# The upper triangle of the decay matrix: select by position on GpSimd in place of a clamp on VectorE

## The chip, the cores and the metric

The kernel runs on one core of one Trainium2 chip. The metric is the device time of one execution in microseconds (us). The engines are named as in the profile: PE (TensorE; PEld its weight loads), DVE (VectorE), ACT (ScalarE), POOL (GpSimd) and SP (SyncE, which issues all DMAs here).

## The reference

Input x is [64, 256, 256] (64 samples of 256 tokens of 256 channels), all in float32. Four layers follow one another, each added to x after a layer norm: a graph attention network with two attention layers (gnn0), a feed-forward block on the 127 best-ranked of 256 tokens (ffn0), another graph attention (gnn1) and a Mamba-2 block (ffn1). The change lies in the last one. With one chunk of 256 tokens its core is

```python
cs = cumsum(dt * A)                       # per head, over the 256 tokens
Lmat[l, s] = exp(cs[l] - cs[s]) if l >= s else 0
Y[l] = sum over s of (C[l] . B[s]) * Lmat[l, s] * x[s] * dt[s]
```

for 8 heads of 64 channels; B and C are shared by the heads. Above the diagonal (l < s) Lmat is zero. There cs[l] - cs[s] is positive and can be large, so that exp of it, if it were taken, could overflow.

## The kernel before

Two samples form a group, so there are 32 groups. The work of a group is cut into lanes, written as Python generators; a step of a lane is what lies between two `yield`s. Lane a is gnn0, b is ffn0 and then gnn1, c is ffn1. The first group's gnn0 is done by halves (lanes a and d, one sample each), and so is the last group's ffn1 (lanes e and f). Lane w loads and prepares weights. Three strings of letters give the order in which the steps are issued: FIRST (305 letters, the start), ORDER (199 letters, repeated 29 times; in each repetition lanes a, b and c of different groups advance by one group), and LAST (403 letters, the end). A letter whose lane can't begin yet is skipped; when LAST's letters have given out, the remaining steps are taken from the lanes in turn. Each engine works through its own instructions in the order of issue.

In ffn1, E holds for each head a tile of 128 partitions (s within a half of the tokens) by 3 blocks of 128 columns (l) per sample: block 0 is s and l in the first half, block 1 is s in the first half and l in the second, block 2 is both in the second. So blocks 0 and 2 hold the diagonal, and block 1 lies wholly below it. E is made as follows:

- cs is written to DRAM (csd) and read back, spread over all partitions (`spread_row`, L809, 264 DMAs). Six buffers of E take turns.
- `decays(h)` clamps blocks 0 and 2 to the value on the diagonal, min(cs[l], cs[s]), with one instruction on DVE (L820; ccs is cs by partition). Then ACT takes exp(E - cs[s]) (L826, two instructions per sample).
- B C^T comes from PE into PSUM (pb), and DVE moves it to cb with a product by tri3 (L891), which is 1 where l >= s and 0 elsewhere.
- DVE multiplies E by cb (L899), and PE takes E into py.

Where the clamp acted, exp gives 1, and tri3's zero in cb removes it.

The convolution of ffn1 is a chain for each m in (4, 0, 1, 2, 3): PE (pp), ACT (L841), three instructions on DVE (L845), ACT (th, L850), DVE (L851); `decays(m)` comes after m = 0 to 3. Later, in the rounds m = 0 to 3, follow L899 for two heads, pz (PE), gz (ACT L907, DVE L908), py (PE), L924 on DVE, L925 on POOL, and for m = 0 and 1 `decays` of two more heads (4 to 7). Other lines that the text names: L489 copies transposed attention weights (at) from PSUM on ACT, L496 and L499 are exps of gnn0 on ACT, L473 scales attention weights on POOL, L567 and L750 are additions on POOL, L671 and L674 are products on DVE in ffn0's gelu, ahead of py there, L594 and L393 are an addition and statistics on DVE. Line numbers of matmuls and transposes are those of two helpers, L251 and L254.

Of the kernel before, what the change touches and what calls it, by code (L numbers as in the profile page):

```python
# [12 lines left out]
ALU = mybir.AluOpType  # L13
AX = mybir.AxisListType

P = 128
# [2 lines left out]
GELU_C = 0.7978845608028654  # L19
GELU_A = 0.044715  # L20
FIRST = (
    "dwddadadwaaadawdaaddadaddaaaaadddaaddaaaaddaddaddadaaadaddaddwawdaaaaaaadddadddawdaaaaadadaadaddbaba"
    "aaabaaaabbaawaaaabwaabaaaaababbbaabbbwababababbbbabaaaabaabaawabababbaaaaabbbaaabbbbabbbaababbababab"
    "baababbbaaaabbabbbabbbaaacwccaababcaababbaabcaaabaaabacabbabbbbbaaabaabaabcbcabaabwbbaacabbaabawabca"
    "bbbab"
)
ORDER = (
    "cAaaccbbbbbbacabaccccbccaabacccabcbccabaacbccacabcaaaacacacbcccccbcacabcccbcaaacacbbccccccacaaccbcac"
    "cbacacabccabcccbcbBabccaccbcccabbcacaacbaccacbcbaacbcbbcbcababcbbcbCccbbbbaacaacabcaabbcbbabbbbbccc"
)  # L30
LAST = (
    "ececefefceecbbceccbbcbffbbbccfcbbfceccebbfcccbefccbcbeceebfcccecccecccceccfbccbcecccbccbeeccbefceccf"
    "ccccccfeeebbccecccfecffffcccfbffebcccbfbceffbccbcccefebbcefcccfceeebcbccccbfefccbcccbfbffcbbccccbcbb"
    "cfceefcbfbbcfefcbbcffbfecccbfcbfefbbbfbfbccffeeeebffbeccccfffebbfebbefbecfcbccccccbcbbcbffcccbeeceec"
    "ebfecbbbbcebffcceccbccccbeccebccececbbefcccffecfccffccfecfebcebceeceecebcffbcfeccfffcfecfeccefcececc"
    "cfe"
)


# [1 line left out]
def kernel(ctx: ExitStack, tc: tile.TileContext, a: dict, out: bass.AP):  # L41
# [5 lines left out]
    nc = tc.nc  # L47
    x = a["x"]
    B, N, D = x.shape
# [19 lines left out]
    def psum(name):  # L69
        return ps.tile([P, 512], F32, tag="ps", name=name)  # L70

    def cons(name, *shape, dt=F32):
        return const.tile(list(shape), dt, tag=name, name=name)
# [16 lines left out]

    ident = cons("ident", P, P)
    make_identity(nc, ident)

    tri3 = cons("tri3", P, 3 * P)
    nc.gpsimd.memset(tri3, 1.0)
    for blk in (0, 2):
        nc.gpsimd.affine_select(
            out=tri3[:, blk * P : (blk + 1) * P],
            in_=tri3[:, blk * P : (blk + 1) * P],
            compare_op=ALU.is_ge,  # L100
            fill=0.0,
            base=0,
            pattern=[[1, P]],
            channel_multiplier=-1,
        )

    before = cons("before", P, 2, N, dt=BF16)
    nc.gpsimd.memset(before, 1.0)
    for c in range(2):
        nc.gpsimd.affine_select(  # L110
            out=before[:, c, :],
            in_=before[:, c, :],
            compare_op=ALU.is_gt,
            fill=0.0,
            base=c * P,
            pattern=[[-1, N]],
            channel_multiplier=1,
# [8 lines left out]
    ones = cons("ones", P, 32)  # L126
# [110 lines left out]
    def tiled(pool, shape, tag, name, bufs):  # L237
        return pool.tile(list(shape), F32, tag=tag, name=name, bufs=bufs)
# [7 lines left out]
    def sized_sm(tag, n, most, *rest, bufs=4):  # L246

        return sm(tag, P, most, *rest, bufs=bufs)[:, :n]
# [117 lines left out]
    def sized(G, own=None):  # L366
# [3 lines left out]
        def wide(make, tag, *rest):  # L370

            if own is None:
                return make(tag, *rest)
            i = taken[tag] = taken.get(tag, -1) + 1
            if i == len(shared.setdefault(tag, [])):
                shared[tag].append(make(tag, *rest))
            return shared[tag][i]
# [374 lines left out]
        def ffn1(xt, of):  # L752
# [6 lines left out]
            r0 = 32 * (own or 0)  # L759
            mine = slice(own or 0, (own or 0) + G)  # L760
            pd = psum("pd")
            for k in range(KD):
# [6 lines left out]
            R = 32 * G  # L769
            dtT, dz, csT = (  # L770
                wide(lambda t: tiled(big, (64, N), t, t, 1), t)[r0 : r0 + R] for t in ("dtT", "dz", "csT")
            )
# [5 lines left out]
            yield  # L778
            nc.vector.scalar_tensor_tensor(dtT, dtT, 0.0, dz, ALU.max, ALU.add)
            nc.vector.tensor_scalar(dz, dtT, negA[r0 : r0 + R], None, ALU.mult)  # L780
            nc.vector.tensor_tensor_scan(csT, tri3[r0 : r0 + R, P : P + 1].to_broadcast([R, N]), dz, 0.0, ALU.mult, ALU.add)


            csd = wide(lambda t: rowd.tile([NH, 2, 3 * P], F32, tag=t, name=t), "csd")[:, mine]
# [11 lines left out]
            ccs = sized_sm("ccs", G, 2, 2, NH, bufs=2)  # L796
# [17 lines left out]
            def decays(h):  # L814

                yield

                e = es[h]
                diag = e.rearrange("p b (k l) -> p b k l", k=3)[:, :, ::2, :]
                nc.vector.tensor_tensor(  # L820
                    diag, diag, ccs[:, :, :, h : h + 1].to_broadcast([P, G, 2, P]), ALU.min
                )
                yield
                for b in range(G):
                    for half, to in enumerate((slice(0, N), slice(N, N + P))):
                        nc.scalar.activation(e[:, b, to], e[:, b, to], AF.Exp, bias=ncs[:, b, half, h : h + 1])  # L826
# [7 lines left out]
            for m in (KI, *range(KI)):  # L834
                yield
                pp = psum("pp")
                for k in range(KD):
                    mm(pp[:, :T], W_in[:, k, DI + m * P : DI + (m + 1) * P], xT[k][:, :T], start=(k == 0), stop=(k == KD - 1))
                yield
                s, pp = columns("xs", "xs"), pp[:, :T]  # L840
                nc.scalar.activation(s, pp, AF.Identity, bias=conv_b[:, m : m + 1], scale=conv_w[:, m, 3:4])  # L841
                s3 = s.rearrange("p (b t) -> p b t", b=G)
                p3 = pp.rearrange("p (b t) -> p b t", b=G)
                for d in range(1, 4):
                    nc.vector.scalar_tensor_tensor(  # L845
                        s3[:, :, d:], p3[:, :, : N - d], conv_w[:, m, 3 - d : 4 - d], s3[:, :, d:], ALU.mult, ALU.add
                    )
                yield
                th = columns("m", "th")
                nc.scalar.activation(th, s, AF.Tanh)  # L850
                nc.vector.scalar_tensor_tensor(s, th, 1.0, s, ALU.add, ALU.mult)  # L851
                xs[m] = s
                if 0 <= m < 4:
                    yield from decays(m)
# [23 lines left out]
            cb = wide(lambda t: tiled(big, (P, 2, 3 * P), t, t, 1), "cb")[:, mine]  # L878
            yield

            pb = [psum("pb") for _ in range(G)]
# [6 lines left out]
                    )  # L888
            yield
            for b in range(G):  # L890
                nc.vector.tensor_tensor(cb[:, b, :], pb[b][:, : 3 * P], tri3, ALU.mult)  # L891
            cb2 = cb.rearrange("p b l -> p (b l)")

            ys = []
            for m in range(KI):
# [16 lines left out]
                for b in range(G):  # L912
                    for half in range(2):
                        for q in range(2):
                            h = 2 * m + q
# [11 lines left out]
                for h in (2 * m + 4, 2 * m + 5):  # L927
                    if len(es) < NH:
                        spread_row()
                    if h < NH:  # L930
                        yield from decays(h)
# [23 lines left out]
            for c in range(C):  # L955
# [5 lines left out]
                nc.vector.scalar_tensor_tensor(xt[:, c, :], po[:, :D], r[:, c : c + 1], xt[:, c, :], ALU.mult, ALU.add)  # L961

        return {f.__name__: f for f in (moments, gnn0, ffn0, gnn1, ffn1)}

    both, one = sized(2), [sized(1, half) for half in range(2)]
# [116 lines left out]
```

## Time and profile before

| | |
|---|---|
| Median of 3 runs | 3652.24 us (3652.19 to 3652.80) |
| Profiled execution: time, span from the first to the last instruction | 3653.81 us, 3652.1 us |
| Mean granted TensorE clock | 0.99 |
| PE busy | 3533.4 us, 97% |
| DVE busy | 2842.1 us, 78% |
| ACT busy | 2189.1 us, 60% |
| POOL busy | 1146.8 us, 31% |
| DMA, mean | 41 GB/s |

Busy times are summed over one profiled execution. PE's instructions are pipelined and their ends are modelled, so a busy PE isn't one at its peak. A stretch of the profile is read by its windows (busy time of each engine in it), by its waits (which engine stood idle, and what ended that), and by the timeline (instructions in order of time, like ones merged, with the idle time before them in brackets).

### The profile page before, as it was taken

What the parts mean: (1) busy time and instruction counts of PE and PEld (TensorE: products, weight loads), DVE (VectorE), ACT (ScalarE), POOL (GpSimd) and SP (SyncE); (2) the same over time, 40 slices, a digit from 0 to 9 for tenths busy, and PEclk for the clock granted to TensorE, in tenths of its full rate; (3) what the DMA queues carried; (4) which work ended last, traced back from release to release, by engine and by line L of the source; (5) the groups of instructions that cost most, each with busy time, mean ns of one, the idle gap of its engine ahead of it and who ended that gap; (6) DMA issues with size and microseconds to landing.
All of it is one profiled execution on the core that took longest, in us unless ns stands there. A gap on an engine that the chain in (4) does not pass through costs nothing.

```text
span 3652.1 us, 50662 instructions
## 1 busy us (share of the span) xinstructions
PE 3533.4 (97%) x17004; PEld 2550.6 (70%) x17004; DVE 2842.1 (78%) x7275; ACT 2189.1 (60%) x4942; POOL 1146.8 (31%) x1274
## 2 busy tenths in 40 slices
PE   8999999999999999999999999999999999999876
PEld 6766776776776776776776776776776777776544
DVE  5577778777778777878777878777878777878776
ACT  4565665665665665666665666655666655666544
POOL 2223333323333323333323333323333323333222
PEclk9999999999999999999999999999999999999989
DMA  3011101111101111101111101111101111101111
GB/s 116 1 39 43 49 15 43 48 42 46 49 15 43 48 40 48 49 15 43 48 40 49 48 16 43 49 40 49 44 20 43 48 40 49 41 23 37 43 43 48
DMA packets 90260, 150.89 MB, mean 41 GB/s; under 512 B 12304, under 2 KB 57232, under 8 KB 90000
## 3 DMA queue, kind: packets, MB, share of 16 engines
q1 hardware_dynamic: 90000, 147.65, 12.1%
q8 instruction: 135, 2.21, 0.2%
q14 instruction: 125, 1.02, 0.1%
HBM read 125.86 MB, written 17.56 MB: 39 GB/s over the span
## 4 chain that ended last, share of the span: by engine, by line
PE 81%; DVE 12%; ACT 4%; issue 1%; POOL 1%; DMA 1%; SPq 0%; ACTq 0%; POOLq 0%; DVEq 0%
PE pp L251 31%; PE u L251 10%; PE py L251 9%; PE po L251 7%; PE pz L251 6%; PE pt L254 5%; PE ph L251 4%; PE pa L251 3%; PE psel L251 2%; DVE st L393 1%; DVE xt L595 1%; DVE g L674 1%; DVE w L498 1%; DVE g L671 1%; DVE w L594 1%; PE pss L251 1%
## 5 line engine op out<-in xcount | busy, mean ns | idle before, releaser
L251 PE MATMUL pp<-W_fc,o 128*128 128x256 f32 (+1 forms) x2048 | 460.1, 379 | 0.4 <-DVE W_fc L286 0.4
L845 DVE SCALAR_TENSOR_TENSOR xs<-pp,conv_w,xs 128x510 f32<-128x510 f32 (+5 forms) x495 | 359.9, 728 | 93.9 <-ACT xs L841 79.9
L251 PEld LDWEIGHTS pp<-W_fc,o 128*128 128x128 f32 x2048 | 381.9, 189 | 67.8 <-issue 15.9
L826 ACT ACTIVATE E<-E,ncs 128x256 f32<-128x256 f32 (+1 forms) x1024 | 382.0, 449 | 61.0 <-DVE E L820 58.3
L473 POOL TENSOR_SCALAR e<-e,den 128x256 f32<-128x256 f32 x384 | 186.8, 505 | 714.2 <-PE pp L251 350.3
L251 PE MATMUL pp<-xT,W_in 128*128 128x512 f32 (+1 forms) x660 | 303.6, 593 | 0.0
L850 ACT ACTIVATE th<-xs 128x512 f32<-128x512 f32 (+1 forms) x165 | 101.7, 617 | 326.6 <-DVE xs L845 311.4
L925 POOL TENSOR_TENSOR xs<-xs,gz 128x512 f32<-128x512 f32 (+1 forms) x132 | 205.9, 1561 | 203.0 <-DVE xs L924 200.5
L251 PE MATMUL py<-w,g 128*128 128x256 f32 x1024 | 236.2, 383 | 20.7 <-DVE g L674 20.7
L899 DVE TENSOR_TENSOR E<-E,cb 128x768 f32<-128x768 f32 (+1 forms) x264 | 250.5, 964 | 1.1
L705 POOL TENSOR_TENSOR xt<-xn,xt 128x512 f32<-128x512 f32 x64 | 81.3, 1270 | 526.1 <-DVE xn L702 525.9
L251 PE MATMUL pz<-xT,W_in 128*128 128x512 f32 (+1 forms) x528 | 242.8, 583 | 0.0
L567 POOL TENSOR_TENSOR o<-w,o 128x512 f32<-128x512 f32 (+1 forms) x132 | 180.7, 1369 | 197.8 <-DVE w L501 197.8
L251 PE MATMUL ph<-sel,w 128*128 128x256 f32 x1024 | 242.0, 379 | 0.0
L251 PE MATMUL po<-W_ol,xs 128*128 128x256 f32 x1024 | 241.3, 379 | 0.0
L251 PEld LDWEIGHTS py<-w,g 128*128 128x128 f32 x1024 | 190.0, 190 | 70.9 <-DVE g L674 46.7
L251 PE MATMUL pp<-xT,mlp_w 128*128 128x512 f32 (+1 forms) x528 | 236.5, 583 | 0.7 <-ACT xT L419 0.7
L251 PE MATMUL u<-at,h 128*128 128x256 f32 x1024 | 236.8, 379 | 0.0
L251 PE MATMUL pp<-o,mlp_w 128*128 128x512 f32 (+1 forms) x528 | 231.1, 590 | 2.9 <-POOL o L567 2.9
L820 DVE TENSOR_TENSOR E<-E,ccs 128x512 f32<-128x512 f32 (+1 forms) x264 | 224.3, 863 | 0.0
L393 DVE BATCH_NORM_STATS2 st<-xt 128x6 f32<-128x256 f32 x512 | 185.1, 413 | 49.7 <-POOL xt L750 23.4
L251 PEld LDWEIGHTS u<-at,h 128*128 128x128 f32 x1024 | 191.7, 190 | 37.6 <-issue 7.3
(179 smaller groups left out, 7722.3 us busy)
## 6 DMA issues: line engine op xcount, KB each, us to landing
E<-csd SPq DMA_DIRECT2D x248, 384.0 KB
xt<-in_x_dram SPq DMA_DIRECT2D x31, 512.0 KB
out_dram<-xt SPq DMA_DIRECT2D x31, 512.0 KB
cs<-xs SPq DMA_DIRECT2D x64, 64.0 KB
E<-csd SPq DMA_DIRECT2D x16, 192.0 KB
w<-in_L_ffn_w_dram SPq DMA_DIRECT2D x2, 1024.0 KB
W_in<-in_L_ffn_W_in_dram SPq DMA_DIRECT2D x1, 1160.0 KB
mlp_w<-in_L_gnn_mlp_w_dram SPq DMA_DIRECT2D x2, 512.0 KB
```

The source lines that it names most:

```text
L251: nc.tensor.matmul(to, lhsT, rhs, start=start, stop=stop)
L254: nc.tensor.transpose(to, of, eye)
L393: nc.vector.bn_stats(st[:, c, :], xt[:, c, :])
L473: nc.gpsimd.tensor_scalar(e, e, den[:, c : c + 1], 1.0, ALU.mult, ALU.mult)
L567: nc.gpsimd.tensor_tensor(o1[m], w, o1[m], ALU.add)
L705: nc.gpsimd.tensor_tensor(pair(xt, b), xn[b], pair(xt, b), ALU.add)
L820: nc.vector.tensor_tensor(diag, diag, ccs[:, :, :, h : h + 1].to_broadcast([P, G, 2, P]), ALU.min)
L826: nc.scalar.activation(e[:, b, to], e[:, b, to], AF.Exp, bias=ncs[:, b, half, h : h + 1])
L845: nc.vector.scalar_tensor_tensor(s3[:, :, d:], p3[:, :, : N - d], conv_w[:, m, 3 - d : 4 - d], s3[:, :, d:], ALU.mult, ALU.add)
L850: nc.scalar.activation(th, s, AF.Tanh)
L899: nc.vector.tensor_tensor(e2, e2, cb2, ALU.mult)
L925: nc.gpsimd.tensor_tensor(yt, yt, gz, ALU.mult)
```

## The change

After it, `decays(h)` issues on POOL, for each sample of the group, one `affine_select` on blocks 0 and 2 of E: where l - s is negative, E becomes -3e38, whatever it was; elsewhere it stays. The exp of that is 0, so cb needs no triangle: L891 becomes a plain copy from PSUM. The tile tri3 and its set-up on POOL go, and the scan that makes cs takes its ones from the tile `ones`. The number of steps in each lane stays, but FIRST, ORDER and LAST hold their letters in another order.

```diff
 FIRST = (
...
 ORDER = (
-    "cAaaccbbbbbbacabaccccbccaabacccabcbccabaacbccacabcaaaacacacbcccccbcacabcccbcaaacacbbccccccacaaccbcac"
-    "cbacacabccabcccbcbBabccaccbcccabbcacaacbaccacbcbaacbcbbcbcababcbbcbCccbbbbaacaacabcaabbcbbabbbbbccc"
+    "Acaccbbbabbcabacccccaccbbbcccaccbcacacaabbcabcacccaaccabbaacacaccccbcbccacbaaccacbacccccacacbaccaaac"
+    "bacabcabcccabcccbacacbBbccbcccccababacbacaacccbbcbabcabccbbabbcbbacbCbbcbcaacaacabcbaabbcbabbbbbccc"
 )
 LAST = (
...
-    tri3 = cons("tri3", P, 3 * P)
-    nc.gpsimd.memset(tri3, 1.0)
-    for blk in (0, 2):
-        nc.gpsimd.affine_select(
-            out=tri3[:, blk * P : (blk + 1) * P],
-            in_=tri3[:, blk * P : (blk + 1) * P],
-            compare_op=ALU.is_ge,
-            fill=0.0,
-            base=0,
-            pattern=[[1, P]],
-            channel_multiplier=-1,
-        )
...
-            nc.vector.tensor_tensor_scan(csT, tri3[r0 : r0 + R, P : P + 1].to_broadcast([R, N]), dz, 0.0, ALU.mult, ALU.add)
+            nc.vector.tensor_tensor_scan(csT, ones[r0 : r0 + R, :1].to_broadcast([R, N]), dz, 0.0, ALU.mult, ALU.add)
...
                 diag = e.rearrange("p b (k l) -> p b k l", k=3)[:, :, ::2, :]
-                nc.vector.tensor_tensor(
-                    diag, diag, ccs[:, :, :, h : h + 1].to_broadcast([P, G, 2, P]), ALU.min
-                )
+                for b in range(G):
+                    nc.gpsimd.affine_select(
+                        out=diag[:, b], in_=diag[:, b], compare_op=ALU.is_ge, fill=-3e38, base=0,
+                        pattern=[[0, 2], [1, P]], channel_multiplier=-1,
+                    )
...
             for b in range(G):
-                nc.vector.tensor_tensor(cb[:, b, :], pb[b][:, : 3 * P], tri3, ALU.mult)
+                nc.vector.tensor_copy(cb[:, b, :], pb[b][:, : 3 * P])
```

More of the change, by code (lines that the diff above doesn't have):

```diff
@@ L21 @@
 FIRST = (
[L22 to L25, printed above, removed]
+    "waaadadddwaadadddaddadaaaaaawdddwaddadaaaaddaddaaadadaaaddddaadaaddaaaddadaddddaaadaaaadaaddadwbaabb"
+    "aaaaawaaaawabaabaaabaaabbaaaaaabbabaabbwbbaaaabaabbbaabbawbbbabbaabaaabaaaaaabwbbbbaabbbbabbbabaaaab"
+    "bbbbbaabaabbbbbabbababbaaabaaabbcbaaaaaabaaaababaaaabbbacwabacacaababwacbbcawacbbbaaabcbaababbcbbaba"
+    "bbbbc"
 )
 ORDER = (
-    "cAaaccbbbbbbacabaccccbccaabacccabcbccabaacbccacabcaaaacacacbcccccbcacabcccbcaaacacbbccccccacaaccbcac"
-    "cbacacabccabcccbcbBabccaccbcccabbcacaacbaccacbcbaacbcbbcbcababcbbcbCccbbbbaacaacabcaabbcbbabbbbbccc"
+    "Acaccbbbabbcabacccccaccbbbcccaccbcacacaabbcabcacccaaccabbaacacaccccbcbccacbaaccacbacccccacacbaccaaac"
+    "bacabcabcccabcccbacacbBbccbcccccababacbacaacccbbcbabcabccbbabbcbbacbCbbcbcaacaacabcbaabbcbabbbbbccc"
 )
 LAST = (
[L32 to L36, printed above, removed]
+    "eefecfebcbecbfeffbecfbcccbcbceccbbcbccfcefbeeccbbcfccbeecccbeececcebcfbccccccfcccfffecebbeccceccbecc"
+    "cfccffbeccfccecccccbcfcceccbcbbeeccfccbbfcbceccebccfcbcebeecfcbffeecbcccccbfcfbbffcbbceffbfbccebcfbe"
+    "bbceefecbcbfbcfcecbcfcbefbbbebfbffceeccefcceeecbfccefbefebfcfccccbbbfbeebefbfcfeccebcbfffccfcfffbeff"
+    "fccbfcecbcbfebccccbcceeccbcccbeecfebeecbbcbcccccbfccccccbbebecefcfcbfccfcbccefcffcfcefecfececcefecfe"
+    "ccf"
 )
```

## The prediction

> **What bounds the kernel now.** I read the page's busy shares and slices first, then the windows, the waits of PE, the groups by form, and the timeline of the last 250 us.
>
> ```profile
> PE 3533.4 (97%) x17004; PEld 2550.6 (70%) x17004; DVE 2842.1 (78%) x7275; ACT 2189.1 (60%) x4942; POOL 1146.8 (31%) x1274
> PE   8999999999999999999999999999999999999876
> PEclk9999999999999999999999999999999999999989
> ```
>
> PE is full in 36 of 40 slices. The four others are the first and the last three, and in the last ones the clock falls too. The windows give sizes (us, then PE, PEld, DVE, ACT, POOL busy, clock, DMA):
>
> ```profile
> 1228.60:1338.33 109.73, 108.78 (x529) 78.65 (x529) 87.68 (x224) 67.81 (x153) 35.83 (x39) 1.00 0.12 41
> 2325.93:2435.67 109.74, 108.79 (x529) 78.65 (x529) 87.66 (x224) 67.80 (x153) 35.84 (x39) 1.00 0.12 40
> 3423.26:3460.00 36.74, 24.11 (x109) 15.24 (x107) 33.17 (x78) 19.85 (x51) 7.65 (x9) 0.81 0.07 22
> 3500.00:3540.00 40.00, 26.70 (x101) 17.13 (x101) 30.80 (x64) 16.66 (x36) 5.62 (x7) 0.85 0.05 17
> 3580.00:3620.00 40.00, 21.50 (x98) 17.15 (x96) 29.68 (x72) 19.53 (x42) 0.00 (x0) 0.79 0.24 77
> ```
>
> The program is a period of 109.73 us, 29 times over (ORDER), between a head of some 240 us and a tail of some 230. In a period PE idles 0.95 us and DVE 22. Over the tail's 229 us (3423 to the end) PE is busy for 163, the three rows above are its idlest, and in them DVE is the fullest engine. Who makes PE wait within one period:
>
> ```profile
> PE py L251 <- DVE g L674: 0.6, 1, 0.6
> PE pst L254 <- ACT ss L944: 0.2, 1, 0.2
> PE pd L251 <- ACT xT L419: 0.2, 1, 0.2
> ```
>
> None of the three is the clamp (L820), so a period has at most 0.95 us to give, 27.6 us over 29. Now what the change exchanges, from the groups by form, and the nearest row of the new operation, from the groups of POOL (the mean in ns stands behind the busy time):
>
> ```profile
> L820 DVE TENSOR_TENSOR E<-E,ccs 128x512 f32<-128x512 f32 x248 | 216.9, 885 | 0.0
> L891 DVE TENSOR_TENSOR cb<-pb,tri 128x384 f32<-128x384 f32 x64 | 32.5, 547 | 0.4 <-PE pb L251 0.3
> L473 POOL TENSOR_SCALAR e<-e,den 128x256 f32<-128x256 f32 x384 | 186.8, 505 | 714.2 <-PE pp L251 350.3 <-ACT w L496 169.7 <-DVE den L468 138.9
> L110 POOL TENSOR_SCALAR_AFFINE_SELECT before<-before 128x256 bf16<-128x256 bf16 x2 | 0.8, 404 | 0.0
> ```
>
> The clamps cost DVE 217 us, and POOL's own row for a select of 256 columns is 404 ns. Last, one round of the two half groups' convolutions in the tail, from the timeline:
>
> ```profile
> 3600.74 0.42 ACT L850 ACTIVATE th<-xs 128x256 f32<-128x256 f32 x1 [1.01 <-DVE xs L845]
> 3601.18 0.42 DVE L851 SCALAR_TENSOR_TENSOR xs<-th,xs 128x256 f32<-128x256 f32 x1 [0.21 <-ACT th L850]
> 3601.53 0.75 DVE L820 TENSOR_TENSOR E<-E,ccs 128x256 f32<-128x256 f32 x2
> 3601.98 1.49 ACT L826 ACTIVATE E<-E,ncs 128x256 f32<-128x256 f32 x4 [0.83 <-DVE E L820]
> 3603.38 1.00 ACT L841 ACTIVATE xs<-pp,conv_b,conv_w 128x256 f32<-128x256 f32 x2
> 3603.96 2.94 DVE L845 SCALAR_TENSOR_TENSOR xs<-pp,conv_w,xs 128x255 f32<-128x255 f32 x6 [1.68 <-ACT xs L841]
> ```
>
> Here the clamp is on the path: ACT waits 0.83 for it, and the next convolution waits for ACT.
>
> **The change, part by part.** *Totals.* 264 clamps (224.3 us) leave DVE. POOL gets 31 x 8 x 2 + 16 = 512 selects of 128x256. A select costs 0.40 (the bf16 row) to 0.51 (f32, another operation): I take 0.42, by the select's own row, 215 us, or 6.7 a period. POOL goes from 35.8 to some 42.5 of 109.73, DVE from 87.7 to some 80.5. Neither was the bound, so in the periods this is worth nothing by itself: PE's 108.78 cover it.
>
> *cb, scan, set-up.* A copy of 384 columns lies between L690's 0.417 (256 columns from PSUM) and today's 0.547, and an input fewer gives no reason for a loss. I take 0.50: 3 us of DVE under PE, 0.3 in the tail. The scan reads ones in place of tri3: nothing. The set-up loses a memset (0.42) and two selects of 0.30 on POOL before 3 us, while DVE waits for x until 4.27: nothing.
>
> *The new chain.* A select needs only E's DMA, not L851 or ccs, so for heads 0 to 3 it can be done before ACT asks. It waits for that DMA at the head of POOL's queue, with L925, L567, L473 and L750 behind it; DVE's clamp stood there with no idle time before it (0.0 in its row), so E was in place, and I add nothing. SP's DMAs keep their number and sizes. For heads 4 to 7 the code issues the select behind L925 on POOL, which waits for L924. The exps that wait for it hold up what is queued on ACT: gz (L907) and the copies L489, and PE waits for those.
>
> *Tail, half groups.* The letters of LAST give out before this stretch in both versions, and the remaining steps run f, e in turn, so the order is the same. In the round above the exps can start when th ends, 3601.16 for 3601.98: 0.82. Two gaps between convolutions gain that; the first gains 0.3, as its E lands at about 3595.7; behind the fourth the path is PE's transposes. Sum -1.9. In the rounds of m, L924 to L924 takes 5.62 (3621.25 to 3626.87), with the first exp 1.60 after L924. With the change: L924 0.55, two L925 of 0.70, a select 0.42 and a step of 0.1 are 2.47, so +0.87 in each of two rounds: +1.7. Bounds 1.6 and 2.9, the upper one if L899, which would then run at that time, slows L925 as it does elsewhere (1.80 in place of 1.28). What is late next is ACT's eight exps (3.05).
>
> *Tail, last two whole groups.* Convolutions of group 30 start at 3499.73, 3506.77, 3513.90 and 3521.62. L851 (0.60) and L820 (0.61) leave the path between th and exps: 0.6 a gap if DVE's queue remains the limit, 1.2 if not. I take 0.9 x 3 = 2.7 there, and 2.2 for group 29, where DVE is 90% busy. Bounds of both together 3.6 and 7.2. Their rounds of m get the later exps (+1.3 at most a round, two each). In group 29's PE has no wait above 0.2 from 3446.8 to 3466.9, which hides it; without that cover it is 2.6. I take +0.7 for group 30's.
>
> *Head.* No clamp starts before 236.9. FIRST is another order of the same steps, and PE idles 23 us there: 0, bounds -2 and +2.
>
> *Sum.* -1.9 + 1.7 - 2.7 - 2.2 + 0.7 - 0.3 = -4.7. With the bounds: about -11 to +5. The profiled execution took 3653.81 (span 3652.10 and 1.7 around it), 1.6 above the median of 3652.24. Against the median: 3647.5. The clock that the tail's rows show (0.79 to 0.85) is taken as it is.
>
> **A rule against it.** Where L820 ran beside L925, the clamp took up to 1.77 against 0.68 alone, and L925 1.66 against 1.28; the two L899 that I found beside one-input L473 took 0.951 against 0.949 alone. So I add nothing for L899 beside selects, outside the rivals. The Trainium skill (SBUF — State Buffer, Who interferes with whom) says that a DVE instruction with two SBUF inputs and a GpSimd instruction that reads SBUF exclude each other, and that the first holds for its whole length. The trace agrees only in part: at 1259.48 the clamp started 0.16 before L925 and still took 1.69. By the rule, each of 8 L899 a period could wait for a select: 8 x 0.42 = 3.4 us more of DVE, still under PE unless they are those ahead of pyE.
>
> **Rivals.** *Slower: PE waits at the copy of at.* In the new ORDER, from the end of head pair 0's py, PE has u, pt, pz, u, pt, py, u ahead of pa: 0.87 + 0.44 + 1.73 + 0.87 + 0.44 + 1.45 + 0.87 = 6.7 us. pa needs L489, and ACT has ahead of it, from 0.9: L496, L489 and L499 (0.5 to 0.65 each), two groups of four exps (1.40 each), L496, L907 and L489 itself: 1.65 + 2.8 + 1.6 = 6.05, so 6.95. With L924, L925 and two selects before the first exps (0.1 + 0.7 + 1.3 + 0.84 = 2.95, where ACT could start at 2.55) it is 7.35. It decides from 6.7 on: every 0.1 beyond is 2.9 us. The present order has that L489 ahead of the exps and no wait there. Price 0.3 to 0.7 a period, up to 1.2 if L899 beside the selects is held up too; 0.6 likely: 29 x 0.6 - 4.7 = +12.7, 3665. Against it: PE may come to that place later than I count, and then nothing waits.
> *Faster: a shorter period.* DVE gets 7 us more slack, and the 0.95 of PE's idle time shrinks. For it: its largest part waits for DVE. Against it: that L674 stands behind L594 and L393, with no clamp within 10 us of it, and both orders have that place nearly alike. Half of it, 0.45 x 29 = 13: 3634.5.
> *Nothing.* The rounds of m cost what the convolutions give: 3652.
>
> **How the numbers follow.** 0.2% is 7.3 us, about what a measurement of this kernel can tell from no change: faster is below 3644.9, slower above 3659.5. Forecast (period within 0.15 either way, head and tail -11 to +5): chance 0.39, own range 3637 to 3657; a third of it lies below 3644.9: 0.13 faster, 0.26 same. Slower rival 0.33: 0.29 slower, 0.04 same. Shorter period 0.22, faster. Nothing 0.06, same. Together 0.35, 0.36, 0.29. The range 3630 to 3672 leaves out some 0.1 at either end.
>
> **What would show it.** L820 gone, 512 selects near 0.42 on POOL, POOL at some 1360 us and DVE near 2610. A period at 109.6 to 109.9, with PE waiting for g L674 as now. No wait of ACT L826 in the half groups' convolutions, which follow one another by 5.4 in place of 6.25, and L924 to L924 at 6.5. I am wrong if a period differs by over 0.2: then PE's waits name pa <- ACT at (slower), or have lost g L674 (faster). Selects over 0.8 would break the POOL part.

## The result: 3663.26 us, 0.26% slower

| | before | after |
|---|---|---|
| Median (10 runs each, lowest to highest) | 3653.65 (3652.19 to 3655.76) | 3663.26 (3658.27 to 3667.40) |
| Profiled execution: time, span | 3653.81, 3652.1 | 3658.27, 3656.6 |

The ratio after to before is 1.0026, with a 95% interval of 1.0016 to 1.0035. The range of 3630 to 3672 holds the time, but the kernel became 9.6 us slower where I forecast 4.7 faster. The profiled execution lies at the low end of the ten times, so its trace shows only some 4.5 us of the loss; the repeated run e1 below shows more.

Line numbers after the change are 11 to 13 lower: L808 is the select, L815 the exp (L826 before), L888 E x cb (L899), L913 and L914 the two steps behind py (L924, L925), L834 to L840 the convolution, L880 the copy to cb (L891), L460 the scaling of e (L473), L661 the product of g (L674). The page, busy time and slices:

```profile
PE 3536.7 (97%) x17004; PEld 2553.3 (70%) x17004; DVE 2663.8 (73%) x7011; ACT 2195.7 (60%) x4942; POOL 1340.6 (37%) x1783
...
PE   8999999999999999999999999999999999999776
...
PEclk9999999999999999999999999999999999999988
```

DVE lost 178 us and POOL gained 194, as announced in kind, and PE's total is as before. One period after the change, the eleventh repetition of ORDER, as a window (length, then PE, PEld, DVE, ACT, POOL busy, clock, DMA) and in PE's waits:

```profile
1324.11:1433.68 109.57, 108.88 (x529) 78.65 (x528) 82.17 (x216) 68.08 (x153) 41.67 (x55) 1.00 0.13 41
```

```profile
PE py L238 <- DVE g L661: 0.5, 1, 0.5
PE pd L238 <- ACT xT L406: 0.2, 1, 0.2
```

The period is 109.57 for 109.73, and no copy of at is waited for. The groups of instructions that the change touches (L815 from the page, the others by form; after the bar busy time, mean ns of one, idle time before):

```profile
L808 POOL TENSOR_SCALAR_AFFINE_SELECT E<-E 128x256 f32<-128x256 f32 x512 | 247.7, 510 | 66.2 <-DMA E<-csd 53.9 <-PE pp L238 11.3
```

```profile
L815 ACT ACTIVATE E<-E,ncs 128x256 f32<-128x256 f32 (+1 forms) x1024 | 379.9, 442 | 39.7 <-POOL E L808 39.7
```

```profile
L888 DVE TENSOR_TENSOR E<-E,cb 128x768 f32<-128x768 f32 x248 | 241.7, 1004 | 0.3 <-issue 0.2
...
L880 DVE COPY cb<-pb 128x384 f32<-128x384 f32 x64 | 32.7, 552 | 0.7 <-PE pb L238 0.6
```

A select takes 0.51 in the mean; by the single records 395 of the 512 take 0.4 and 59 take 1.1, all 59 beside L888. The copy costs as much as the product did (0.552 for 0.547).

PE's matmuls (all 17004 are in both traces) tell where each string begins and ends. Lengths in us:

| stretch | before | after | e1 | e2 | e4 | e8 | e12 |
|---|---|---|---|---|---|---|---|
| FIRST | 218.5 | 221.2 | 222.4 | 218.2 | 216.1 | 218.0 | 216.9 |
| 29 x ORDER | 3181.5 | 3181.9 | 3182.4 | 3241.3 | 3179.0 | 3180.2 | 3181.4 |
| one of its 27 inner periods (median) | 109.73 | 109.58 | 109.57 | 111.79 | 109.58 | 109.64 | 109.73 |
| LAST | 178.8 | 182.2 | 183.6 | 180.7 | 178.7 | 173.7 | 172.4 |
| steps behind LAST (half groups) | 66.5 | 65.2 | 67.7 | 69.8 | 68.0 | 67.8 | 66.6 |

After the change 27 inner periods give 3.2 us back, and their two neighbours, which adjoin the new FIRST and LAST, take 1.4 and 2.3 more each. FIRST and LAST lose 2.7 and 3.4 (in e1, 4.0 and 4.8). FIRST is counted from PE's first matmul, which the new letters bring 0.7 earlier (at 6.1 for 6.8), so ORDER begins 1.9 later than before, and 3.2 in e1. In the head, where no select has run yet, PE's waits from 120 to 180 us were 2.7 for L473 before; after:

```profile
PE pt L241 <- POOL e L460: 7.2, 4, 6.3
```

In the half groups the convolutions are as forecast and the rounds of m are not (timeline after, one round):

```profile
3623.45 1.04 DVE L913 SCALAR_TENSOR_TENSOR xs<-xs,Dcol,py 128x256 f32<-128x256 f32 x2
...
3624.01 1.73 POOL L914 TENSOR_TENSOR xs<-xs,gz 128x256 f32<-128x256 f32 x2 [23.21 <-DVE xs L913]
...
3624.41 3.09 DVE L888 TENSOR_TENSOR E<-E,cb 128x384 f32<-128x384 f32 x4
...
3625.69 2.43 POOL L808 TENSOR_SCALAR_AFFINE_SELECT E<-E 128x256 f32<-128x256 f32 x4
...
3626.45 2.88 ACT L815 ACTIVATE E<-E,ncs 128x256 f32<-128x256 f32 x8 [3.70 <-POOL E L808]
...
3630.29 0.86 DVE L913 SCALAR_TENSOR_TENSOR xs<-xs,Dcol,py 128x256 f32<-128x256 f32 x2
```

The first exp comes 3.00 behind L913 (1.60 before), the next L913 6.84 (5.62 before). Between the two stand both L914 and the first select. The four L888 take 3.09 beside them; the four L899 before, with nothing beside them on POOL, took 1.95 (from 3624.28).

### The profile page after: what moved, and what is told of

Same layout as the page of the kernel before. It is cut to its first block, busy times and chain, and to the rows that moved or that the text cites. A ratio compares the mean times of both kernels' runs of the same rounds, so it can differ in the third digit from the quotient of the medians.

```text
span 3656.6 us, 51663 instructions
## 1 busy us (share of the span) xinstructions
PE 3536.7 (97%) x17004; PEld 2553.3 (70%) x17004; DVE 2663.8 (73%) x7011; ACT 2195.7 (60%) x4942; POOL 1340.6 (37%) x1783
## 4 chain that ended last, share of the span: by engine, by line
PE 81%; DVE 12%; ACT 5%; issue 1%; POOL 1%; DMA 0%; SPq 0%; POOLq 0%; ACTq 0%; DVEq 0%
PE pp L238 31%; PE u L238 11%; PE py L238 9%; PE po L238 7%; PE pz L238 6%; PE pt L241 5%; PE ph L238 4%; PE pa L238 3%; PE psel L238 2%; DVE st L380 1%; DVE xt L582 1%; DVE g L661 1%; PE fb L241 1%; DVE g L658 1%; ACT w L483 1%
## 5 line engine op out<-in xcount | busy, mean ns | idle before, releaser
L238 PE MATMUL pp<-W_fc,o 128*128 128x256 f32 (+1 forms) x2048 | 468.1, 381 | 0.0
L834 DVE SCALAR_TENSOR_TENSOR xs<-pp,conv_w,xs 128x510 f32<-128x510 f32 (+5 forms) x495 | 359.9, 728 | 79.6 <-ACT xs L830 67.0
L460 POOL TENSOR_SCALAR e<-e,den 128x256 f32<-128x256 f32 x384 | 181.4, 490 | 619.0 <-DVE den L455 403.3
L815 ACT ACTIVATE E<-E,ncs 128x256 f32<-128x256 f32 (+1 forms) x1024 | 379.9, 442 | 39.7 <-POOL E L808 39.7
L808 POOL TENSOR_SCALAR_AFFINE_SELECT E<-E 128x256 f32<-128x256 f32 x512 | 247.7, 510 | 66.2 <-DMA E<-csd 53.9
L888 DVE TENSOR_TENSOR E<-E,cb 128x768 f32<-128x768 f32 (+1 forms) x264 | 252.9, 989 | 0.3 <-issue 0.2
L914 POOL TENSOR_TENSOR xs<-xs,gz 128x512 f32<-128x512 f32 (+1 forms) x132 | 167.2, 1268 | 233.9 <-DVE xs L913 233.9
L238 PE MATMUL u<-at,h 128*128 128x256 f32 x1024 | 247.2, 385 | 0.3 <-ACT at L476 0.3
L656 POOL TENSOR_SCALAR g<-g 128x512 f32<-128x512 f32 x128 | 82.6, 645 | 403.2 <-ACT g L655 403.0
L485 DVE TENSOR_SCALAR w<-w 128x512 f32<-128x512 f32 (+1 forms) x196 | 114.6, 585 | 154.6 <-ACT w L483 154.6
L380 DVE BATCH_NORM_STATS2 st<-xt 128x6 f32<-128x256 f32 x512 | 185.2, 414 | 50.3 <-POOL xt L692 23.9
```

Source lines behind the costliest of these rows:

```text
L238: nc.tensor.matmul(to, lhsT, rhs, start=start, stop=stop)
L380: nc.vector.bn_stats(st[:, c, :], xt[:, c, :])
L460: nc.gpsimd.tensor_scalar(e, e, den[:, c : c + 1], 1.0, ALU.mult, ALU.mult)
L485: nc.vector.tensor_scalar(w, w, 1.0, None, ALU.min)
L656: nc.gpsimd.tensor_scalar(g, g, 8 * GELU_A * GELU_C, 2 * GELU_C, ALU.mult, ALU.add)
L808: nc.gpsimd.affine_select(out=diag[:, b], in_=diag[:, b], compare_op=ALU.is_ge, fill=-3e38, base=0, pattern=[[0, 2], [1, P]], channel_mult ...
```

## The experiments

Ratios are to the kernel before, run on the same chip (its medians there 3653.9 to 3654.5). Times in us.

| run | letters (FIRST, ORDER, LAST) | operations | median | ratio and interval |
|---|---|---|---|---|
| e1 | new | new | 3665.5 | 1.0030 [1.0019, 1.0042] |
| e2 | old | new | 3716.3 | 1.0170 [1.0153, 1.0187] |
| e3 | new | old | 3855.2 | 1.0551 [1.0535, 1.0566] |
| e4 | old, new, old | new | 3652.7 | 0.9999 [0.9989, 1.0008] |
| e5 | old, new, new | new | 3661.3 | 1.0022 [1.0013, 1.0031] |
| e13 | new, new, old | new | 3659.4 | 1.0014 [1.0005, 1.0023] |
| e6 | new | selects 4 to 7 ahead of L914 | 3661.7 | 1.0019 [1.0010, 1.0028] |
| e7 | old | the same | 3649.7 | 0.9987 [0.9978, 0.9996] |
| e8 | old, new, old | the same | 3646.7 | 0.9979 [0.9970, 0.9988] |
| e9 | old, new, old | no selects 4 to 7 | 3643.6 | 0.9970 [0.9959, 0.9982] |
| e11 | old, new, old | selects 4, 5 earlier still | 3653.9 | 0.9999 [0.9990, 1.0008] |
| e10 | new | each select twice | 3738.8 | 1.0231 [1.0217, 1.0245] |
| e12 | old | selects 0 to 3 alone | 3646.8 | 0.9980 [0.9971, 0.9989] |

**Operations or letters (e1 to e4).** The change is two changes: other operations, and other letters. Theory O held that the letters of FIRST and LAST cost it all and the selects nothing; theory S that the selects, waiting on POOL for E's DMA, hold up what stands behind them. e1 is the changed kernel again. The others swap whole strings and leave the operations:

```diff
 # e2: the kernel after
-FIRST, ORDER, LAST of after
+FIRST, ORDER, LAST of before
 # e3: the kernel before
-FIRST, ORDER, LAST of before
+FIRST, ORDER, LAST of after
 # e4: the kernel after
-FIRST, LAST of after
+FIRST, LAST of before
```

> The changed kernel unchanged, for the spread of its own times and a second profile. In its first profile, against the kernel before: head up to the end of the first repetition of ORDER +3.3 us, 27 repetitions -3.0 together, last repetition and LAST's steps +5.7, the two half groups' end -1.3. Theory O (the letters: what is lost is lost by the new FIRST and LAST, the selects cost nothing) and theory S (the selects: they wait on POOL for E's DMA and hold up what stands behind them) both expect 3658 to 3667 here; S expects that a slower execution shows later landings of E ahead of its longer periods.

> Selects and the plain copy, with FIRST, ORDER and LAST of the kernel before. Theory O: head 0, repetitions 109.7 each, LAST's steps 0 to -5, half groups' end -1.3: 3646 to 3652. Theory S: LAST's steps and the last repetition keep their +5.7: 3655 to 3662, and executions spread by some 9 us as after the change.

> The clamp on DVE and the product with the triangle, with FIRST, ORDER and LAST of the changed kernel. Theory O: head +3.3, LAST's steps +6 or more, repetitions 109.6 to 110.3: 3660 to 3680. Theory S: 3648 to 3654, with executions within 4 us of one another.

> The changed kernel with FIRST and LAST of the kernel before and the new ORDER. Theory O: repetitions 109.58, so -4, head 0, LAST's steps 0 to -5, half groups' end -1.3: 3642 to 3649, faster than both. Theory S: 3654 to 3662.

e4 gave the whole loss back, as O says in kind, though not the further 4 to 11 us that O expected of it (3642 to 3649 for 3652.7). But e2 refutes O's other half: in the old order the selects cost 2.06 a period, 62 us in all, more than S expected too. In e3, far above both expectations, the clamp in the new order costs 6.4 a period (PE waits 4.1 for L540 there); I did not follow that up. So operations and ORDER belong together: where the selects stand in the queue here, they are free only if the letters leave room for them. What a select does in the old order, e2's timeline shows (DVE, POOL and ACT in order of time):

```profile
1388.90 0.75 DVE L913 SCALAR_TENSOR_TENSOR xs<-xs,Dcol,py 128x512 f32<-128x512 f32 x1
...
1389.73 1.91 POOL L914 TENSOR_TENSOR xs<-xs,gz 128x512 f32<-128x512 f32 x1
...
1391.60 2.38 POOL L808 TENSOR_SCALAR_AFFINE_SELECT E<-E 128x256 f32<-128x256 f32 x4
...
1392.22 0.80 ACT L815 ACTIVATE E<-E,ncs 128x256 f32<-128x256 f32 x2 [1.70 <-POOL E L808]
...
1393.30 2.18 ACT L815 ACTIVATE E<-E,ncs 128x256 f32<-128x256 f32 x6 [0.27 <-POOL E L808]
...
1395.39 0.71 ACT L486 ACTIVATE w<-w,neg 128x512 f32<-128x512 f32 x1
...
1396.48 0.58 ACT L896 ACTIVATE gz<-pz 128x512 f32<-128x512 f32 x1
...
1397.09 0.69 DVE L897 SCALAR_TENSOR_TENSOR gz<-gz,pz 128x512 f32<-128x512 f32 x1 [0.27 <-ACT gz L896]
...
1398.38 0.73 DVE L913 SCALAR_TENSOR_TENSOR xs<-xs,Dcol,py 128x512 f32<-128x512 f32 x1
```

The selects of heads 4 and 5 stand behind L914 on POOL. ACT stands 1.70 and 0.27 for them, and gz (L896) of the next round is queued behind those exps. So L913 follows L913 by 9.48; in the same place before it was 7.64:

```profile
1368.55 0.75 DVE L924 SCALAR_TENSOR_TENSOR xs<-xs,Dcol,py 128x512 f32<-128x512 f32 x1
...
1376.19 0.75 DVE L924 SCALAR_TENSOR_TENSOR xs<-xs,Dcol,py 128x512 f32<-128x512 f32 x1
```

PE then meets the late E (e2, waits in one period):

```profile
PE py L238 <- DVE E L888: 1.5, 1, 1.5
```

**The place of the selects (e6, e7, e8).** From here theory Q: the price of heads 4 to 7 is their place behind L914. Theory C: it is select and L888 slowing each other, wherever they meet. The edit is the same in all three, with after's letters (e6), before's (e7), and e4's (e8):

```diff
-    def decays(h): yield; select(h); yield; exps(h)
+    def decays(h): yield; if h < 4: select(h)
+                   yield; exps(h)
...
     nc.vector.scalar_tensor_tensor(yt, yt, Dcol[:, m : m + 1], py[:, :T], ALU.mult, ALU.add)
+    for h in (2 * m + 4, 2 * m + 5):
+        if h < NH: select(h)
     nc.gpsimd.tensor_tensor(yt, yt, gz, ALU.mult)
```

> The changed kernel with its own letters; only the place of one kind of instruction differs: the selects of heads 4 to 7 are issued ahead of L914 of the same round on POOL in place of behind it. Theory Q (in the rounds of m the selects stand behind L914, and the first exp comes 3.9 us after L913's start in place of 1.5): the first exp comes some 1 us after L913, the rounds of m in LAST and in the half groups fall by 1 to 2.4 us each, and the time falls by 4 to 8 us, 3657 to 3661. Theory C (what costs is that select and E*cb of L888 slow each other, 0.40 to 1.13 and 0.95 to 2.02, wherever they meet): the meeting only moves, and the time stays at 3662 to 3667.

> The new operations with all three strings of before, as e2, with the selects of heads 4 to 7 ahead of L914. In e2 a period is 111.79, with one wait of PE at py for E of L888 (1.5) that is in no period of before. Theory Q: that wait is the chain L913, L914, select, exp, E*cb; it goes, the period is 109.6 to 109.9 again, and the time falls from 3716 to 3645 to 3655. Theory C: part of the 2.06 stays, period over 110.5, time over 3675.

> As e4 (new operations, new ORDER, FIRST and LAST of before), with the selects of heads 4 to 7 ahead of L914. Theory Q: LAST's rounds of m lose the 2 us each that e4 shows against before (L913 to L913 8.9 and 8.8 for 6.5 and 6.9), the half groups' rounds 1.2 each: 5 to 7 us less than e4's 3652.7, 3645 to 3648, faster than both kernels. Theory C: 3651 to 3655.

e7 settles it for the periods: with nothing but those selects moved, the time falls from 3716.3 to 3649.7 and the period from 111.79 to 109.80. Theory C does not account for that: E x cb is as often slow in e7 as in e2 (over 1.05 us in 62 and 63 of its 248 records of 128x768), and selects over 1.05 us are more (61 for 33). In the tail, e4 and e8 have the same letters. POOL in the same two rounds of LAST, the kernel before first, then e4:

```profile
3449.22 1.71 POOL L925 TENSOR_TENSOR xs<-xs,gz 128x512 f32<-128x512 f32 x1
3455.65 1.65 POOL L925 TENSOR_TENSOR xs<-xs,gz 128x512 f32<-128x512 f32 x1 [4.71 <-DVE xs L924]
```

```profile
3441.92 1.97 POOL L914 TENSOR_TENSOR xs<-xs,gz 128x512 f32<-128x512 f32 x1
3443.84 2.20 POOL L808 TENSOR_SCALAR_AFFINE_SELECT E<-E 128x256 f32<-128x256 f32 x4
3450.78 1.91 POOL L914 TENSOR_TENSOR xs<-xs,gz 128x512 f32<-128x512 f32 x1 [4.74 <-DVE xs L913]
3452.64 2.20 POOL L808 TENSOR_SCALAR_AFFINE_SELECT E<-E 128x256 f32<-128x256 f32 x4
```

and e8, where L922 is L914, L893 is L888 and L805 the select:

```profile
3444.81 2.92 POOL L805 TENSOR_SCALAR_AFFINE_SELECT E<-E 128x256 f32<-128x256 f32 x4
3447.70 1.27 POOL L922 TENSOR_TENSOR xs<-xs,gz 128x512 f32<-128x512 f32 x1
3448.92 1.49 POOL L805 TENSOR_SCALAR_AFFINE_SELECT E<-E 128x256 f32<-128x256 f32 x4
```

The selects that took 2.20 behind L914 in round two are done at 1.49, 0.9 us before the round's L913 (3451.30). L913 to L913 in these rounds, by the records: 6.49 and 6.85 before, 8.87 and 8.80 in e4, 7.30 and 5.97 in e8. Behind these rounds PE waits for the late E in e4 (waits from 3458 to 3464); in e8 and before it has no wait there:

```profile
PE py L238 <- DVE E L888: 2.5, 2, 1.3
```

LAST falls by 5.0, the total by 6.0, though over the whole kernel E x cb is slowed more often than in e4 (33 of its records over 1.5 us, 5 in e4). In the half groups the two rounds fall as well (from 6.84 and 6.90 to 4.84 and 5.98), but their stretch stays (67.8 for 68.0), at a granted clock of 0.82 for 0.87.

e6's gain is 1.6 (on after) to 3.8 (on e1), less than the 4 to 8 expected, and its 3661.7 lies between the two theories: its half groups gained (64.3 for 65.2 and 67.7); in LAST PE idles 3.5 less (43.2 for 46.7), but the stretch is longer (185.6), at a granted clock of 0.86.

**How far it goes (e9, e11).** The same letters as e4 and e8:

```diff
-    select(h)                                                 (e9: for h >= 4)
-    nc.scalar.activation(..., AF.Exp, bias=ncs[:, b, half, h : h + 1])
+    nc.scalar.activation(..., AF.Exp, bias=neg1, scale=1e-6)
...
+    if m == 3: select(4); select(5)                           (e11: in the loop of convolutions, behind decays(3))
```

> As e4 (new operations, new ORDER, FIRST and LAST of before), but heads 4 to 7 have no select; so that nothing overflows, their exp takes E x 1e-6 - 1 in place of E - cs. It leaves out 256 of the 512 selects and the true exponent of these heads. It bounds what those selects cost where e8 has them, ahead of L914. Theory Q (they cost only by the place in the queue): 3644 to 3648, within 3 us of e8's 3646.7, with LAST's PE idle time at e8's 40.4 less 1 to 2 for the first round, in which e8's selects stand in the way of L914. Theory C (they slow E*cb wherever they are): over 4 us below e8, under 3643.

> As e8, with the selects of heads 4 and 5 issued earlier still, behind the exps of head 3 (their E is sent for with the first six); those of heads 6 and 7 stay ahead of L914. In e8's first round of m POOL comes late from L473's place (its L460), the four selects take 2.9 us beside E*cb (0.73 each in place of 0.40) and L914 starts 3.7 us after L913. Theory Q: that round shortens by 1 to 2 us in LAST's two groups and in the half groups: 3642 to 3646, under e8's 3646.7. Rival (POOL then waits for E's DMA earlier and holds up L460, L554 or L737 in the periods): period over 109.8 and 3650 or more.

Without any select of heads 4 to 7, e9 is 3.2 below e8. In the traces the half groups are 3.7 shorter (64.1 for 67.8) and ORDER 1.5; LAST is 0.9 longer (174.6 for 173.7), with the same idle time of PE (40.3 and 40.4). That is between the two expectations: most of the price was the place, some 3 us remain. e11 fell on the rival's side: 3653.9. Its period is 109.83, and matmul by matmul it loses 0.20 to e8's at one place, fb behind L702 on DVE; its LAST (173.9) gained nothing. Why L702 came later I did not test, so the rival's reason isn't shown: POOL waits hardly longer for E's DMA (60.7 in all, 57.3 in e8). That e11 is 7.1 slower than e8 though only 5 of its E x cb take over 1.05 us (64 in e8) speaks against C once more.

**Slack and the first half alone (e10, e12).**

```diff
     for b in range(G): nc.gpsimd.affine_select(out=diag[:, b], ...)
+    for b in range(G): nc.gpsimd.affine_select(out=diag[:, b], ...)      (e10, after's letters)
```

```diff
-    nc.vector.tensor_tensor(diag, diag, ccs[...].to_broadcast([P, G, 2, P]), ALU.min)
+    if h < 4: select(h)                                                   (e12, the kernel before, triangle kept)
+    else: nc.vector.tensor_tensor(diag, diag, ccs[...].to_broadcast([P, G, 2, P]), ALU.min)
```

> The changed kernel with each select issued twice, 512 more of 0.41 to 1.1 us on POOL, 6.7 to 8 us more a period; a second select changes nothing in E. It shows what slack POOL and the chain behind L914 have left. Theory Q: in the periods PE's work still covers it, period 109.5 to 109.9; the rounds of m in LAST and the half groups take 0.8 to 1.5 more each, 5 to 8 in all: 3669 to 3675. Rival (the chain has no slack left in ORDER's place either): period 110.2 or more, time above 3682.

> The kernel before, all its letters, with one part of the change alone: selects for heads 0 to 3 (in the convolutions), the clamp for heads 4 to 7 and the triangle in cb kept. Theory Q: nothing stands behind L925, so no 2.06 as in e2: period 109.6 to 109.9; the convolutions of LAST and of the half groups gain 2 to 5 in all: 3649 to 3652 beside 3654. Rival (selects in the convolutions cost a period too, for they wait on POOL for E's DMA): period over 110, 3662 or more.

e10's rival was right: 111.82 a period, 3738.8. As in e2, PE waits at py for a late E in each period (1.2, in two waits). So the new ORDER has no room for a second select on each, though POOL is busy for only 42 of 109.6 us in after, and some 49 of 111.8 in e10. e12 is faster than its expectation: the period stays at 109.73, LAST is 6.4 shorter. Its selects take 0.409 each, and what POOL waits for is only E:

```profile
L822 POOL TENSOR_SCALAR_AFFINE_SELECT E<-E 128x256 f32<-128x256 f32 x256 | 97.0, 409 | 60.9 <-DMA E<-csd 60.7
```

Half of the change, on the old letters, is 7.6 us faster than the kernel before. It ties with e8 as the fastest version that leaves nothing out; the intervals of both lie below 1 and below that of after.

**Which letters (e5, e13).** Each undoes one string of after:

```diff
-FIRST of after      (e5)      -LAST of after      (e13)
+FIRST of before               +LAST of before
```

> The changed kernel with FIRST as it was before (ORDER and LAST new). In the changed kernel's head PE waits 6.3 us at one place (pt behind L460 on POOL, at 120 us, when no select has run yet) where the kernel before waits 2.7. Theory L (the letters of FIRST cost 4 us of the loss by themselves, no select takes part): the stretch of FIRST falls by 3 to 6 us, the time from 3665 to 3659 to 3662. Rival (the head loses by something else, or the stretch behind it gives the loss back): 3664 to 3667.

> The changed kernel with LAST as it was before (FIRST and ORDER new). e4 (old FIRST and LAST) took 3652.7, e5 (old FIRST alone) 3661.3, the changed kernel 3663.3 and 3665.5: by these LAST's letters cost 8.6 and FIRST's 2 to 4. Theory L (the two add up, each by its own stretch): 3655 to 3658, with O28 at 109.8 and PE's idle time in LAST near e4's 44.2. Rival (LAST's 8.6 was only the stretch's granted clock, which differs from run to run, and not its letters): 3661 to 3666.

With neither new string (e4) 3652.7, with LAST's alone (e5) +8.6, with FIRST's alone (e13) +6.7, with both +10.5 to +12.8. So either string costs by itself, and the two don't add up. e5 came as its theory said; e13 is above the 3655 to 3658 of its theory (its last repetition of ORDER, O28 in the text above, takes 109.6 as expected), and its interval overlaps e4's a little, so FIRST's share is the less certain. Of the 9.1 by which e13's trace is longer than e4's, 4.7 lie ahead of ORDER and 1.1 in it. The other 3.3 lie in LAST and behind it, where the letters are the same, and where PE even idles less in LAST (40.5 for 44.2), at a granted clock of 0.86 for 0.89. The wait of 6.3 in the head goes with FIRST's letters: PE idles 26.7 to 26.9 us up to ORDER in after, e1, e6, e10 and e13, and 23.0 to 23.9 in the runs with the old FIRST. POOL waits there for den from DVE, and PE for POOL; no select takes part (after, timelines of POOL and of PE):

```profile
126.14 1.84 POOL L460 TENSOR_SCALAR e<-e,den 128x256 f32<-128x256 f32 x4 [3.62 <-DVE den L455]
```

```profile
126.67 2.05 PE L241 MATMUL pt<-ident,e 128*128 128x128 f32 x8 [6.34 <-POOL e L460]
```

LAST's length is not its idle time alone. In after, e1 and e5 PE idles 46.7 to 46.9 in it, and it lasts 182.2, 183.6 and 187.1: the granted clock is 0.90, 0.89 and 0.87. The whole time moves with the clock: of after's ten executions the three with a mean of 0.991 took 3658.3 to 3661.7, the three with 0.989 took 3666.4 to 3667.4. What sets the clock in one execution stays open, and with it some 5 us of scatter. So it is only in part known how LAST's letters cost their 8.6. In the traces of e5 and e4, 2.3 are the last repetition of ORDER (112.06 for 109.77) and 2.6 PE's idle time in LAST (46.9 for 44.2). Another 5.7 there are PE's busy time (140.2 for 134.5) at a lower clock (0.87 for 0.89), and whether the letters bring that about isn't shown.

## Why the prediction was wrong

*Periods: right in number, for the wrong reason.* 109.58 lies within 0.15 of 109.73, and PE waits where I said. But the reason, that POOL and DVE are not the bound and PE's 108.78 cover the selects, is refuted by e2 (+2.06) and e10 (+2.24). It is the new ORDER that makes room, so the number came true by luck; POOL's share of 38% said nothing about how late its results come.

*Convolutions: right.* I took -2.2 for group 29 and -2.7 for group 30. First to last th took 24.95 and 25.63 before and 22.72 and 22.78 in e4: -2.2 and -2.9; e12, without the rounds' selects, keeps all of it. (After's own LAST splits the gain another way: 24.24 and 21.66.) In the half groups th follows th by 5.32 (5.4 forecast), over three gaps 2.8 less in after (1.9 forecast). With the old LAST one of them grew to 7.3 (e4) and 7.7 (e12) from 6.25, as the select waited for E's DMA there (5.70 idle on POOL in e12): "I add nothing" for that wait was wrong in this place, and 53.9 us of it stand in L808's row.

*Rounds of m: the step that failed.* "Which hides it" for group 29, +0.7 for group 30 and +1.7 for the half groups make +2.4. With the old letters (e4) the rounds took +2.4 and +2.0 (group 29), +1.6 (group 30) and +1.2 twice (half groups), +8.4 in all, and ate the convolutions' gain. The half groups' +2.4 lies within my bounds (1.6 to 2.9); for the whole groups I had set +1.3 as the most for a round. I had priced the chain through L925 and two selects only for the rival and for the half groups, and had taken PE's full stretch before as a cover. The cover was too short: in e4 PE has no wait above 0.3 from 3436 to 3460, and then the 2.5 shown above. The rival's mechanism was right (late exps hold up ACT's queue), its place was not: gz and L913 of the next round, not the copy of at, and in the old ORDER (e2), not in the new one, for which I had priced it.

*L899 beside selects: nothing added, and the ground for it was misread.* L888 takes 0.95 alone, 1.15 beside selects and 2.02 beside L914 and then a select; a select takes 0.40 alone and 1.13 beside L888 (in the half groups 0.55, 0.75, 1.08, and 0.40, 0.72). I had set that aside on two records of one-input L473 and on the clamp at 1259.48. But the row of 2.37 us at that time was two clamps merged; by narrower windows of the timeline before:

```profile
1259.48 0.68 DVE L820 TENSOR_TENSOR E<-E,ccs 128x512 f32<-128x512 f32 x1
...
1259.64 1.65 POOL L925 TENSOR_TENSOR xs<-xs,gz 128x512 f32<-128x512 f32 x1
...
1260.08 1.77 DVE L820 TENSOR_TENSOR E<-E,ccs 128x512 f32<-128x512 f32 x1
```

The first clamp took the 0.68 that it takes alone, and L925 and then the second clamp waited their turn. The same in e4's first round:

```profile
3441.75 1.01 DVE L888 TENSOR_TENSOR E<-E,cb 128x768 f32<-128x768 f32 x1
3441.92 1.97 POOL L914 TENSOR_TENSOR xs<-xs,gz 128x512 f32<-128x512 f32 x1
...
3442.68 2.02 DVE L888 TENSOR_TENSOR E<-E,cb 128x768 f32<-128x768 f32 x1
...
3443.84 1.13 POOL L808 TENSOR_SCALAR_AFFINE_SELECT E<-E 128x256 f32<-128x256 f32 x1
```

Each ends after the one that began before it, and the four, 0.95 + 1.27 + 0.95 + 0.40 = 3.6 alone, take 3.2 together (3441.75 to 3444.97). A record holds its wait, so the second and later ones look long. The Trainium skill (SBUF — State Buffer, Who interferes with whom) has such a pair exclude each other. The records agree, the length of the first included: in after's trace all 58 L888 of 1.15 end 0.81 after the select that began before them, and those that begin before a POOL instruction keep 0.92 to 0.96. What these turns cost where e8 has them is little: e9, almost without them, is 3.2 faster.

*Head and LAST's letters: the other failed step.* "Another order of the same steps: 0, bounds -2 and +2" was +1.9 (after) and +3.2 (e1) where ORDER begins, with 3.7 more idle time of PE (26.9 for 23.1). In e13's trace it is 4.7 against e4's (e13's whole time is 6.7 above e4's). For LAST's new letters I had no term at all, and they cost 8.6 by e5 against e4. This is the largest part of the miss: with the old ends the same change is even (3652.7).

*Sizes.* Selects 0.51, not 0.42, for 59 of them meet L888. The copy saves nothing (0.552, 0.50 forecast). POOL 1341 (1360 forecast), DVE 2664 (2610 forecast). POOL's total is near only because two misses cancel: the selects take 248 for 215, and L914, which no longer meets the clamp, takes 1.30 in the mean for L925's 1.61.

## What to carry to other kernels

Moving work to an idle engine is priced by the queue it joins: ask what stands ahead of it there, who waits for its result, and what is queued behind that waiter; the engine's busy share doesn't tell. Where the moved instruction needs less than its neighbour, issue it ahead of the neighbour: here that one move was worth 67 us in one order, 6 in another and 2 to 4 in a third. And when a change comes with a new order of issue, cost the order as a change of its own, its ends above all, where no period averages a wait away.

## What was not expected of the hardware

A product of two SBUF tensors on DVE and a select on POOL, which reads one, took strict turns, and the wait stands in the records as length: the select at up to nearly three times its own (0.40 to 1.13), the product at 1.15 for 0.95. A copy of 384 columns from PSUM took as long as the product with an SBUF tensor (0.552 and 0.547). And three executions with the same order of LAST and the same idle time of PE differed by up to 4.9 us there, with the granted clock at 0.87 to 0.90.
